# A graph attention layer walked in eight streams: the last tile's spreads of q put ahead of three one-hot tables, and the end's transfers shared out to POOL's queue

## The chip, the cores and the metric

The kernel runs on one core of a Trainium2 chip. Its engines work at the same time and wait for one another by semaphores: TensorE (PE in the profile) multiplies matrices into PSUM, VectorE (DVE) and ScalarE (ACT) work on SBUF and PSUM, GpSimd (POOL) and SyncE (SP) mostly issue transfers here. SP, ACT and POOL each issue transfers from a queue of their own. The metric is the time of one execution on the device in microseconds (us).

## The reference

One graph attention layer with a normalization ahead of it and the input added at its end: 12500 nodes of 256 numbers, 200000 edges sorted by destination, 8 heads of D = 32, everything in 32-bit floats.

```python
h = jnp.maximum(_layernorm(x, axis=-1), 0.0)
...
q = (x @ Wq + bq).reshape(n, HEADS, D)
k = (x @ Wk + bk).reshape(n, HEADS, D)
v = (x @ Wv + bv).reshape(n, HEADS, D)
logits = jnp.einsum('ehd,ehd->eh', q[dst], k[src]) / jnp.sqrt(jnp.float32(D))
seg_max = jax.ops.segment_max(logits, dst, num_segments=n)
expv = jnp.exp(logits - seg_max[dst])
denom = jax.ops.segment_sum(expv, dst, num_segments=n)
attn = expv / denom[dst]
agg = jax.ops.segment_sum(attn[:, :, None] * v[src], dst, num_segments=n)
out = agg.reshape(n, HID) + (x @ Wskip + bskip)
h = jax.nn.gelu(out, approximate=False)
y = x + h
```

The layer runs on h (its x is this h), y is normalized with gamma and beta, and the first x is added to it. The destinations are drawn as the square of a uniform number, so low nodes have many edges and high ones few.

## The kernel before

A first stage of some 205 us writes two tables to device memory: kv_tab, a row of 512 numbers (key and value) for each node, and h_tab, the normalized input. The change does not touch it.

The rest is `walk_streams`. The sorted edges are cut into S = 8 streams that are walked side by side. A step c takes K = 3 tiles of 128 edges from each stream, and there are 66 steps; the loop's body is written out 65 times (c = 0 to 64), and the last body breaks off halfway into the code of the end. Within a step the work on tile j goes as follows.

- Gather: for each of the 8 streams one indirect transfer on POOL's queue brings the 128 key and value rows of its edges (L1340, 262 KB). `gather_next` puts the 8 rows of a later tile on a list and has the first one issued behind a DVE instruction (`weigh`). The others are taken from the list one at a time by `turns(latest[PE])`, which stands behind each of the TensorE groups below: the gather then waits for that group's last matmul. When the list is empty, such a call does nothing. So the order in which TensorE's groups are written sets which gather waits for what.
- Windows and queries: `windows` fetches the 64 nodes that a stream may meet in this step from h_tab (SP), `turn_windows` transposes them (L1302, copied to hwT by ACT, L1306), and `queries` multiplies them with Wq (L1316, L1320, copied to qw by ACT, L1323).
- One-hot tables: `hot_e(c, i)` for i = 0 to 3 makes, by one matmul (L1366) and a relu on ACT (L1369), the table to_e of which edge belongs to which node of the window, two streams each. `hot_n` (L1379, L1382) makes the table for the way back.
- Spread: `spread(c, j, half)` multiplies qw with to_e (8 matmuls of 64 rows, L1392), so that each edge has its query, in one of two PSUM tiles ps_qe. Then `times` multiplies it with the gathered keys on DVE (L1402), `total` sums over a head's numbers (L1409), and `turn` transposes the logits (L1428).
- Softmax and sums: `maxima` runs two scans over the logits on DVE (L1440, L1441), ACT takes the exponential, `turn_back` transposes back (L1450), `weigh` multiplies the values (L1477), `add_up` sums them by node with to_n (L1500) and stores the sums to a table in device memory (L1522).

Tiles overlap: while step c is weighed and added up, the spreads and products of step c + 1 run, and the tables, queries and gathers of step c + 2 are made.

From a step on, `Pair`s of node blocks are finished beside the walk, one in each step (the first is due in step 18; the loop finishes one in 45 steps): `fetch` (sums, x and h by SP, L1056 to L1058), `turn`, `skip` and `add` (h times Wskip and the divided sums, in PSUM), `gelu` (ACT, L1097), `stats` and `root` (DVE, then a square root on ACT, L1113), in the next step `factors`, `normal`, `shifted`, `scale` and `store` (L1168). ACT loads a table (L1262) whenever it goes from one of gelu, square root and exponential to another.

Nothing schedules this: instructions run on each engine in the order in which the code is written. The piece of the loop's body that the change moves about is the middle one, between the first tile's `gather_next` and the second tile's.

At the end, after the last two steps, four `Half` pairs (`early_two` and `last`) and two whole ones (`before` and `older`) are left. A `Half` gets its rows in four pieces of 64 nodes, with one transfer each for h, x and sums (L1206, L1210, L1214) and one for each piece of the result. The sums of `last` can be fetched only when the last stores of the walk are done.

Of the kernel before, what the change touches and what calls it, by code (L numbers as in the profile page):

```python
# [38 lines left out]
DVE = mybir.EngineType.DVE  # L39
PSUM = bass.MemoryType.PSUM  # L40
DRAM = bass.MemoryType.DRAM

P = 128
# [943 lines left out]
def walk_streams(tc, N, HID, NST, KL, many, ident, idx, d0_row, slot_row, near, near_n, e_tab, pen_tab, h_tab,  # L987
# [39 lines left out]
    class Pair:  # L1027
# [4 lines left out]
        def __init__(self, pool, m, ps_h, ps_o, keep):  # L1032
            self.pool, self.m, self.ps_h, self.ps_o, self.keep = pool, m, ps_h, ps_o, keep

# [125 lines left out]

        def store(self, b, queue=nc.sync):
            if b == 0:
                self.nodes = loaded(slot_row[0:1, self.m, 0:2], N - P)
            self.put(out[ds(self.nodes[b], P), :], self.y[:, b, :], queue)
# [11 lines left out]
    class Half(Pair):  # L1176
# [26 lines left out]
        def fetch_h(self):  # L1203
            self.places()
            for t, node in zip(self.parts(self.h), self.nodes):
                self.keep(nc.sync.dma_start(t, self.rows_of(h_tab, node)))  # L1206
# [5 lines left out]
        def fetch_sums(self, group=None):  # L1212
            for t, row in zip(self.parts(self.sums), self.rows):
                ins = self.keep(nc.sync.dma_start(t, self.rows_of(tab, row)))  # L1214
                if group:
                    tc.add_to_no_dep_group(group, ins.ins)
# [11 lines left out]
    with ExitStack() as es:  # L1228
# [388 lines left out]
        for c in range(NST - 1):  # L1617
# [10 lines left out]
            if c == NST - 2:  # L1628
                last_nodes = places(0, N - P, (SP, ACT))
                last_rows = places(2, S * NT - P, (SP, ACT))  # L1630
# [60 lines left out]
            if pair:  # L1691
                table_of(AF.Gelu)
                pair.divide()
            if pair_next:
                pair_next.fetch()
            if before:
                before.store(1)
# [103 lines left out]
        last[0].fetch_x(nc.scalar)  # L1801
# [37 lines left out]
        for p in last:  # L1839
            p.shifted()  # L1840
        for p in [older] + done:
# [366 lines left out]
```

## Time and profile before

| | |
|---|---|
| median of 3 runs | 2704.53 us (2700.92 to 2709.87) |
| the profiled execution | 2724.49 us, its span 2722.4 us |
| mean granted clock of TensorE | 0.815 |
| busy, from 300 to 860 us (560 us) | PE 385.8, DVE 364.2, ACT 157.8, POOL 356.5 us |
| busy, from 1300 to 2500 us (1200 us) | PE 883.1, DVE 852.7, ACT 529.1, POOL 726.6 us |
| mean share of the DMA engines in these two | 0.70 and 0.75 |

The first stretch lies in the steps without a pair, the second in those with one. A row of the timeline gives the start, the duration, the engine, the line and the operation, and in brackets how long the engine idled just before and what ended it; "x16" are 16 instructions in one row. A row of a group (those with a "|") gives the total busy time and the mean of one in ns, then the idle time before all of them and the largest share of it by releaser.

### The profile page before, as it was taken

The page shows a single profiled execution, that of the slowest core. Times are in us where ns is not written, and L with a number is a line of the kernel's source. Part 1 is how long each engine was busy: PE and PEld are TensorE (multiplying, and loading weights), DVE is VectorE, ACT ScalarE, POOL GpSimd, SP SyncE. Part 2 cuts the span into 40 slices and gives each one's busy share as a digit, 9 for nine tenths or more (in the row PEclk, how much of TensorE's full clock was granted, in tenths as well). Part 3 has the DMA queues.
Part 4 walks back from the last instruction along what each step waited for, and adds up shares of the span by engine and source line. Part 5 has one row for each costly group of instructions (what it writes and reads, how often), then busy time and mean ns, then how long its engine had stood idle before and what let it go on. Part 6 is the DMA issues. An engine that isn't in the chain of part 4 may idle for free.

```text
span 2722.4 us, 36232 instructions
## 1 busy us (share of the span) xinstructions
PE 1982.6 (73%) x10159; PEld 1181.6 (43%) x10159; DVE 1869.3 (69%) x2165; ACT 1100.8 (40%) x2576; POOL 1620.4 (60%) x1741
## 2 busy tenths in 40 slices
PE   9994567677677677677766777777777777777776
PEld 4442344344444444444444444444444444444443
DVE  8872666666666667766767677776677767776776
ACT  5741222222222244444444444444444444444444
POOL 5456566666666665666556556656656666565652
PEclk9996777877777788888888887888888888888878
DMA  9786566777676777777777777777777777777773
GB/s 348 287 292 196 170 200 203 208 211 206 202 206 204 217 224 217 210 220 228 221 215 213 220 220 221 219 224 225 231 218 219 220 221 229 217 216 213 230 210 108
DMA packets 278904, 596.02 MB, mean 219 GB/s; under 512 B 53040, under 2 KB 166852, under 8 KB 275616
## 3 DMA queue, kind: packets, MB, share of 16 engines
q0 software_dynamic: 128224, 421.39, 53.5%
q1 hardware_dynamic: 148996, 170.91, 19.4%
q8 instruction: 83, 1.36, 0.2%
q10 hardware_dynamic: 1472, 1.31, 0.2%
q14 instruction: 129, 1.06, 0.1%
HBM read 510.92 MB, written 82.47 MB: 218 GB/s over the span
## 4 chain that ended last, share of the span: by engine, by line
PE 43%; another core or an unknown queue 14%; issue 13%; DVE 12%; ACT 11%; POOL 3%; DMA 2%; SPq 2%; DVEq 0%; POOLq 0%; ACTq 0%
PE ps_qe L1392 9%; PE ps_a L1088 6%; PE ps_a L1500 5%; PE ps_hot L1320 5%; ACT kv L1517 4%; DVE vw L1477 4%; PE ps_kv L340 4%; DVE kv L1402 3%; DVE L L1409 2%; PE ps_hot L1500 2%; POOL kv L1340 2%; ACT sums_w L1513 2%; ACT to_n L1382 2%; PE ps_hot L1153 2%
## 5 line engine op out<-in xcount | busy, mean ns | idle before, releaser
L1340 POOL DMA_INDIRECT kv<-kv_tab,idx x1520 | 1454.5, 957 | 926.3 <-issue 370.1
L1402 DVE TENSOR_TENSOR kv<-ps_qe,kv 128x1024 f32<-128x1024 f32 x392 | 466.6, 1219 | 587.5 <-remote 266.2
L1392 PE MATMUL ps_qe<-qw,to_e 64*128 64x256 f32 x3136 | 526.1, 476 | 216.2 <-issue 116.4
L1477 DVE TENSOR_TENSOR vw<-ps_x,kv 128x2048 f32<-128x2048 f32 x194 | 442.0, 2278 | 151.2 <-ACT vw L1466 123.7
L1392 PEld LDWEIGHTS ps_qe<-qw,to_e 64*128 64x128 f32 x3136 | 384.6, 234 | 370.8 <-issue 259.0
L1409 DVE TENSOR_REDUCE L<-kv 128x64 f32<-128x2048 f32 x196 | 447.7, 2284 | 5.1
L1323 ACT COPY qw<-ps_hot 128x256 f32<-128x256 f32 (+1 forms) x132 | 63.2, 479 | 601.6 <-PE ps_hot L1320 322.3
L1320 PE MATMUL ps_hot<-w_q,hwT 128*128 128x256 f32 x792 | 246.9, 456 | 19.2 <-ACT hwT L1306 18.8
L1500 PE MATMUL ps_a<-vw,to_n 128*32 128x264 f32 (+1 forms) x2304 | 237.0, 433 | 23.4 <-ACT kv L1517 18.3
L1320 PEld LDWEIGHTS ps_hot<-w_q,hwT 128*128 128x128 f32 x792 | 164.5, 222 | 117.7 <-issue 70.1
L1306 ACT COPY hwT<-ps_hot 128x256 f32<-128x256 f32 (+1 forms) x132 | 63.3, 480 | 360.4 <-PE ps_hot L1302 189.7
L340 PE MATMUL ps_kv<-w_kv,hT 128*128 128x512 f32 x392 | 184.5, 594 | 1.0 <-ACT hT L254 0.7
L1262 ACT ACT_TABLE_LOAD x139 | 178.3, 1283 | 2.6
L1088 PE MATMUL ps_a<-w_s,hT 128*128 128x256 f32 x360 | 167.7, 645 | 11.2 <-issue 4.8
L1379 PE MATMUL ps_hot<-near_n,et 48*128 48x384 bf16 x196 | 63.0, 376 | 143.3 <-ACT to_n L1382 139.3
L1366 PE MATMUL ps_hot<-et,near 48*128 48x384 bf16 x264 | 93.0, 353 | 91.7 <-ACT ps_x L1431 44.8
L1369 ACT ACTIVATE to_e<-ps_hot,ones 128x384 f32<-128x384 f32 x264 | 142.8, 581 | 10.4 <-PE ps_hot L1366 8.6
L1500 PEld LDWEIGHTS ps_a<-vw,to_n 128*32 128x32 f32 (+1 forms) x2304 | 95.2, 127 | 112.6 <-ACT kv L1517 39.6
L1517 ACT COPY kv<-ps_a 1x264 f32<-1x264 f32 x384 | 141.5, 368 | 6.3
L1088 PEld LDWEIGHTS ps_a<-w_s,hT 128*128 128x128 f32 x360 | 112.5, 328 | 58.7 <-issue 29.7
L1123 ACT ACTIVATE sums<-sums,nm,rstd 128x256 f32<-128x256 f32 x90 | 49.1, 592 | 211.0 <-DVE nm L1118 120.5
L1513 ACT COPY sums_w<-ps_a 128x264 f32<-128x264 f32 x128 | 48.4, 378 | 202.1 <-remote 74.7
(327 smaller groups left out, 2334.6 us busy)
## 6 DMA issues: line engine op xcount, KB each, us to landing
kv<-kv_tab,idx POOLq DMA_INDIRECT x1568
kv_tab<-kvo SPq DMA_DIRECT2D x23, 1024.0 KB
hw<-h_tab SPq DMA_DIRECT2D x264, 64.0 KB
table<-sums_w SPq DMA_DIRECT2D x260, 61.9 KB
pen<-pen_tab SPq DMA_DIRECT2D x66, 192.5 KB
sums<-table SPq DMA_DIRECT2D x92, 132.0 KB
x_in<-in_x_dram SPq DMA_DIRECT2D x23, 512.0 KB
h_tab<-h SPq DMA_DIRECT2D x23, 512.0 KB
```

Source lines behind the costliest of these rows:

```text
L340: nc.tensor.matmul(ps_kv, hT[:, c, :], w_kv[:, c, :], start=c == 0, stop=c == KC - 1)
L1088: self.keep(nc.tensor.matmul(self.ps[:, b, :], self.hT[:, b, c, :], w_s[:, c, :], start=False, stop=False, skip_group_check=True))
L1262: keep(nc.scalar.activation(dummy[:, 1:2], dummy[:, 0:1], function))
L1320: keep(nc.tensor.matmul(ps[:, b, :], g["hwT"][:, b, k, :], w_q[:, k, :], start=False, stop=k == KC - 1, skip_group_check=True))
L1340: ins = nc.gpsimd.indirect_dma_start(out=t[:, s, :], out_offset=None, in_=kv_tab[:, :], in_offset=bass.IndirectOffsetOnAxis(ap=idx[:, s, j ...
L1369: keep(nc.scalar.activation(step[c]["to_e"][:, i, :], ps[:, :CH], AF.Relu, scale=-1.0, bias=ones))
L1392: keep(nc.tensor.matmul(ps[:, b, a, :], g["to_e"][r, 2 * half + a, j * P:(j + 1) * P], g["qw"][r, (half + a) * half, :], start=True, stop= ...
L1402: keep(nc.vector.tensor_tensor(k, g["qe", half].rearrange("p b a d -> p a b d"), k, op=OP.mult))
L1409: keep(nc.vector.tensor_reduce(g["L"][:, j, :].rearrange("p (s h) -> p s h", s=S), g["kv"][j][:, :, :HID].rearrange("p s (h d) -> p s h d" ...
L1477: keep(engine.tensor_tensor(t[:, :, HEADS:].rearrange("p s (h d) -> p s h d", h=HEADS), wj[:, :, :, None].to_broadcast([P, t.shape[1], HEA ...
L1500: keep(nc.tensor.matmul(ps[at:at + w, :], g["to_n"][:, j, i * P + at:i * P + at + w], g["vw"][j][:, s, :], start=j == 0, stop=j == tiles_o ...
L1517: keep(copy(step[c + 1]["kv"][0][0:1, s, HID - HEADS:], ps[at:at + 1, :]))
```

## The change

In the walk's step, four things are written in another place. The store of the second block of a finished pair stands ahead of the next pair's fetches. `pair.add` stands behind the first queries, and `pair.gelu` behind the second ones. The three calls hot_e(c + 2, 1) to (c + 2, 3) stand behind the two spreads of the last tile of step c + 1. No instruction of the step is added or taken away.

The places in the list of gathers go with the order. For the first tile of step c + 2, row 0 still waits for `weigh`, and rows 1 to 5 for the first queries, `turn`, `turn_windows`, hot_e 0 and the second queries. Rows 6 and 7 waited for hot_e 1 and hot_e 2; they now wait for the first and the second half of the spread. The three calls behind them find the list empty.

At the end, several transfers change their queue: x of `last[0]` goes from ACT's to POOL's, x and sums of `last[1]` from SP's to POOL's, the eight stores of `early_two` from SP's to POOL's; of the eight stores of `last`, which SP and ACT had half each, SP has the four of `last[0]`, ACT and POOL two each of `last[1]`. The stores of `before` stand ahead of the fetches of sums of `last`, h of `last[1]` ahead of the sums of `early_two`; the loop around the gelus takes the pairs in another order, with `shifted` behind it; and the nodes that `before` and `older` are stored to are read earlier (`found`).

```diff
-            if pair_next:
-                pair_next.fetch()
             if before:
                 before.store(1)
-            if pair:
-                pair.add()
+            if pair_next:
+                pair_next.fetch()
             if c + 2 < NST:
                 queries(c + 2, 0)
             if pair:
-                pair.gelu()
+                pair.add()
             turn(c + 1, 0)
             if c + 2 < NST:
                 turn_windows(c + 2, 1)
                 hot_e(c + 2, 0)
                 queries(c + 2, 1)
-                for i in range(1, S // 2):
-                    hot_e(c + 2, i)
+            if pair:
+                pair.gelu()
             for half in range(2):
                 times(c + 1, 1, half)
                 spread(c + 1, K - 1, half)
+            if c + 2 < NST:
+                for i in range(1, S // 2):
+                    hot_e(c + 2, i)
             total(c + 1, 1)
...
+        last[1].fetch_h()
         for p in early_two:
             p.fetch_sums("whole")
-        last[1].fetch_h()
+        for p in (before, older):
+            p.found(keep)
...
-        last[0].fetch_x(nc.scalar)
+        last[0].fetch_x(nc.gpsimd)
...
-        last[1].fetch_x()
-        for p in last:
-            p.fetch_sums()
         for b in range(2):
             before.store(b)
+        last[0].fetch_sums()
+        last[1].fetch_sums(queue=nc.gpsimd)
+        last[1].fetch_x(nc.gpsimd)
...
-        for p in last:
-            p.shifted()
-        for p in [older] + done:
+        for p in (older, early_two[0], last[0], early_two[1], last[1]):
...
                 for part in range(2 if p is older else 4):
-                    p.store(part)
+                    p.store(part, nc.sync if p is older else nc.gpsimd)
+        for p in last:
+            p.shifted()
...
-                p.store(part, (nc.sync, nc.scalar)[part // 2])
+                p.store(part, nc.sync if p is last[0] else (nc.scalar, nc.gpsimd)[part // 2])
```

What this does to TensorE's order in a late step: first before, from the second queries (L1320) over the one-hot matmuls 1 to 3 (L1366, from the constant near and the step's et) to the two halves of the spread (L1392) and the transpose of logits (L1428). The loads of weights between them are left out.

```order
L1316 MATMUL ps_hot_9825<-b_q3_70,one_row_69 128x512
L1320 MATMUL ps_hot_9825<-w_q_68,hwT_9818 128x256 x4
L1366 MATMUL ps_hot_9833<-et_9572,near_84 128x384
L1366 MATMUL ps_hot_9837<-et_9572,near_84 128x384
L1366 MATMUL ps_hot_9841<-et_9572,near_84 128x384
L1392 MATMUL ps_qe_9845<-qw_9499,to_e_9518 128x256 x4
L1392 MATMUL ps_qe_9851<-qw_9499,to_e_9518 128x256 x4
L1428 MATMUL ps_x_2267<-ident_62,L_9770 64x128
```

The same place after, where five lines are added ahead in the file (L1325, L1371, L1397 and L1433 are those calls).

```order
L1321 MATMUL ps_hot_9824<-b_q3_70,one_row_69 128x512
L1325 MATMUL ps_hot_9824<-w_q_68,hwT_9817 128x256 x4
L1397 MATMUL ps_qe_9834<-qw_9497,to_e_9517 128x256 x4
L1397 MATMUL ps_qe_9841<-qw_9497,to_e_9517 128x256 x4
L1371 MATMUL ps_hot_9847<-et_9572,near_84 128x384
L1371 MATMUL ps_hot_9850<-et_9572,near_84 128x384
L1371 MATMUL ps_hot_9853<-et_9572,near_84 128x384
L1433 MATMUL ps_x_2267<-ident_62,L_9770 64x128
```

The spread, whose qw and to_e belong to the step before, comes right behind the queries, and the three one-hot matmuls stand between it and the transpose.

On ACT in the same step, before: the copies of the queries (qw) and of the transposed windows (hwT), the gelu (L1097), the relus that make to_e, and the square root (L1113) behind a table load.

```order
L1323 COPY qw<-ps_hot 128x256
L1097 ACTIVATE sums<-ps_a 128x512
L1431 COPY ps_x<-M 64x1
L1306 COPY hwT<-ps_hot 128x512
L1369 ACTIVATE to_e<-ps_hot,ones 128x384
L1323 COPY qw<-ps_hot 128x512
L1369 ACTIVATE to_e<-ps_hot,ones 128x384 x3
L1262 ACT_TABLE_LOAD
```

And after:

```order
L1328 COPY qw<-ps_hot 128x256
L1436 COPY ps_x<-M 64x1
L1311 COPY hwT<-ps_hot 128x512
L1374 ACTIVATE to_e<-ps_hot,ones 128x384
L1328 COPY qw<-ps_hot 128x512
L1099 ACTIVATE sums<-ps_a 128x512
L1374 ACTIVATE to_e<-ps_hot,ones 128x384 x3
L1267 ACT_TABLE_LOAD
```

The gelu has gone behind the copies that the second queries and the products wait for. The three relus keep their place in ACT's order, but the matmuls that they read now stand behind the spread.

More of the change, by code (lines that the diff above doesn't have):

```diff
@@ L39 @@
 DVE = mybir.EngineType.DVE
+POOL = mybir.EngineType.Pool
 PSUM = bass.MemoryType.PSUM
@@ L1033, in __init__ @@
             self.pool, self.m, self.ps_h, self.ps_o, self.keep = pool, m, ps_h, ps_o, keep
+            self.nodes = None
         def places(self):
@@ L1628, in walk_streams @@
             if c == NST - 2:
-                last_nodes = places(0, N - P, (SP, ACT))
-                last_rows = places(2, S * NT - P, (SP, ACT))
+                last_nodes = places(0, N - P, (SP, ACT, POOL))
+                last_rows = places(2, S * NT - P, (SP, POOL))
                 for each in (c, c + 1):
@@ L1693, in walk_streams @@
                 pair.divide()
+            if before:
+                before.store(1)
             if pair_next:
                 pair_next.fetch()
-            if before:
-                before.store(1)
-            if pair:
-                pair.add()
             if c + 2 < NST:
```

14 lines of the change are left out of this document (8 added, 6 removed).

## The prediction

> **What bounds the kernel now.** I read the page first: busy shares, chain, costliest groups.
>
> ```profile
> PE 1982.6 (73%) x10159; PEld 1181.6 (43%) x10159; DVE 1869.3 (69%) x2165; ACT 1100.8 (40%) x2576; POOL 1620.4 (60%) x1741
> PE 43%; another core or an unknown queue 14%; issue 13%; DVE 12%; ACT 11%; POOL 3%; DMA 2%; SPq 2%; DVEq 0%; POOLq 0%; ACTq 0%
> L1340 POOL DMA_INDIRECT kv<-kv_tab,idx x1520 | 1454.5, 957 | 926.3 <-issue 370.1
> L1402 DVE TENSOR_TENSOR kv<-ps_qe,kv 128x1024 f32<-128x1024 f32 x392 | 466.6, 1219 | 587.5 <-remote 266.2
> ```
>
> No engine is full. What stands out is line L1402, the products of gathered keys with spread queries: DVE idles 587.5 us ahead of it, and 266.2 us of that has no releaser the page can name ("remote"; on one core it means only that). So I went to the timeline of one late step, engine by engine.
>
> ```profile
> 1512.33 0.68 DVE L1100 TENSOR_TENSOR sums<-sums,h 128x512 f32<-128x512 f32 x1
> 1520.76 2.36 DVE L1402 TENSOR_TENSOR kv<-ps_qe,kv 128x1024 f32<-128x1024 f32 x2 [6.75 <-remote]
> 1523.04 0.15 DVE L1117 RECIPROCAL rstd<-rstd 128x2 f32<-128x2 f32 x1
> 1529.08 0.95 DVE L1440 TENSOR_TENSOR_SCAN ps_x<-pen,ps_x 64x384 f32<-64x384 f32 x1
> ```
>
> ```profile
> 1510.50 1.99 PE L1320 MATMUL ps_hot<-w_q,hwT 128*128 128x256 f32 x8
> 1512.42 0.33 PE L1366 MATMUL ps_hot<-et,near 48*128 48x384 bf16 x1
> 1513.65 0.32 PE L1366 MATMUL ps_hot<-et,near 48*128 48x384 bf16 x1 [0.16 <-issue]
> 1513.66 2.04 PE L1392 MATMUL ps_qe<-qw,to_e 64*128 64x256 f32 x16
> 1515.86 1.10 PE L1500 MATMUL ps_a<-vw,to_n 128*32 128x264 f32 x16
> 1522.04 3.76 PE L1392 MATMUL ps_qe<-qw,to_e 64*128 64x256 f32 x16 [5.09 <-DVE kv L1402]
> 1527.83 0.30 PE L1428 MATMUL ps_x<-ident,L 128*64 128x128 f32 x1 [0.44 <-DVE vw L1477]
> ```
>
> ```profile
> 1514.13 0.95 POOL L1340 DMA_INDIRECT kv<-kv_tab,idx  x1 [0.31 <-issue]
> 1515.38 0.95 POOL L1340 DMA_INDIRECT kv<-kv_tab,idx  x1 [0.30 <-issue]
> 1516.63 0.95 POOL L1340 DMA_INDIRECT kv<-kv_tab,idx  x1 [0.30 <-issue]
> 1517.88 0.95 POOL L1340 DMA_INDIRECT kv<-kv_tab,idx  x1 [0.30 <-issue]
> 1521.12 0.94 POOL L1340 DMA_INDIRECT kv<-kv_tab,idx  x1 [2.29 <-remote]
> 1524.40 0.95 POOL L1340 DMA_INDIRECT kv<-kv_tab,idx  x1 [1.08 <-PE ps_qe L1392]
> 1528.05 1.15 POOL L1340 DMA_INDIRECT kv<-kv_tab,idx  x1 [1.02 <-DVE vw L1477]
> ```
>
> The spread of the last tile (16 matmuls of 64 rows) is recorded from 1513.66 to 1515.70, yet DVE, with nothing else to do, takes up its products only at 1520.76, 7.1 us after that start. At about the same time POOL, which had issued gathers 1.25 us apart (0.95 and a 0.30 gap) and then waited, goes on (1521.12). The last gather of that burst ended at 1517.88 + 0.95 = 1518.83; DVE was released 1.93 us later. My reading is that such a spread is completed late while gathers are in flight, and is let go when POOL runs out of released rows and its queue drains. That is a reading, not a row.
>
> In the early steps, where no pair is finished, POOL's rows show the same beat without gaps:
>
> ```profile
> 566.65 0.94 POOL L1340 DMA_INDIRECT kv<-kv_tab,idx  x1 [2.10 <-remote]
> 578.40 0.95 POOL L1340 DMA_INDIRECT kv<-kv_tab,idx  x1 [2.05 <-remote]
> 587.16 0.95 POOL L1340 DMA_INDIRECT kv<-kv_tab,idx  x1 [0.30 <-issue]
> 590.19 0.95 POOL L1340 DMA_INDIRECT kv<-kv_tab,idx  x1 [2.08 <-PE ps_qe L1392]
> ```
>
> Eight gathers, a pause of 2.05 to 2.10, eight more. A step has 24 gathers: 24 x 1.25 + 3 x (2.07 - 0.30) = 35.3 us. The rows 566.65 and 590.19 lie 23.5 apart, two thirds of that. So early steps are bound by POOL's issuing plus three pauses; late ones by DVE's and TensorE's waits, with POOL having some slack.
>
> **The change, part by part: the walk's step.** Three things follow from the order shown above.
>
> (1) The spread goes ahead of three one-hot matmuls (hot_e). It would start at 1512.42 in place of 1513.66: 1.24 us earlier. The gelu leaves its place ahead of the copy of hwT on ACT, for which the query matmuls wait:
>
> ```profile
> 1508.98 0.60 ACT L1097 ACTIVATE sums<-ps_a 128x512 f32<-128x512 f32 x1
> 1509.47 0.16 ACT L1431 COPY ps_x<-M 64x1 f32<-64x1 f32 x1
> 1513.01 1.57 ACT L1369 ACTIVATE to_e<-ps_hot,ones 128x384 f32<-128x384 f32 x3
> 1514.60 1.28 ACT L1262 ACT_TABLE_LOAD   x1
> 1516.01 0.28 ACT L1113 ACTIVATE rstd<-mv,eps 128x2 f32<-128x2 f32 x1
> ```
>
> That is another 0.49 (1508.98 to 1509.47): 1.73 together. DVE's statistics (1512.33) then wait about a microsecond for the gelu, in time in which DVE idles 6.75 now: nothing, as long as that wait stays above 1 us. pair.add moves behind the first queries on TensorE, the store of an output row ahead of six fetches on SP: the gelu reads the former 3 us later than now, the fetched rows are for the next step. Both nothing.
>
> (2) Rows of the gather queue are released one by one by TensorE instructions as they are written. For the tile being gathered, rows 6 and 7 are released now by hot_e 1 and 2; afterwards by the two halves of the spread. POOL's rows at 1515.38 and 1516.63 are these, and 1517.88 (the next tile's row 0) queues behind them. So POOL's burst ends three gathers earlier, 3 x 1.25 = 3.75 us, at 1515.08; with the same 1.93 the release comes at 1517.0, not 1520.76. Three gathers are left for later: POOL has issued them by 1517.3 + 3 x 1.25 = 1521.0, where it starts the next row now (1521.12). POOL loses nothing there.
>
> (3) hot_e 1 to 3 come behind the late spread, and with them their three relus on ACT, and behind these a table load and the root. The second half of the spread is done some 1.0 after the first (half of 2.04): 1518.0. Then 1.57 for the relus, 1.41 from table load to root (1514.60 to 1516.01), 0.28: the root is there at 1521.3. DVE's reciprocal of it stands at 1523.04 now, and comes right behind the products. So of the 3.75 us only 1.7 are left at that point.
>
> (4) Next on TensorE comes add_up (1515.86 now), then the next step's first spread (1522.04 now). It can start when add_up is through: 1519.0 for the last hot_e, 0.3 for the transpose, 1.1, so 1520.4, 1.6 earlier. But it now starts with gathers in flight, where before it had POOL's pause. Its neighbours bound this: as released at 1524.40 now (first half 2.1 us after its start with two gathers in flight) the 1.6 are kept; late as the other spread is, until POOL waits for it and drains, it is done near 1526.5, not 1525.8, and the transpose at 1527.83, on which the scan at 1529.08 depends, comes 0.8 later. I take 0.8 us gained: the row at 1524.40 is the nearest (the same spread), with half of its gain taken off for three more gathers in flight. Ends: -1.7 and +0.8.
>
> Steps that finish a pair: 45. 45 x -0.8 = -36 (ends -77 and +36).
>
> Early steps, 18: POOL bounds them, so only its pauses count. Rows 6 and 7 behind the spread move a pause from behind the next tile's row 0 to ahead of row 6. If the next spread then needs no pause of its own, it stays at three: 0. One more costs 2.05 - 0.30 = 1.75 a step; the earlier release may give up to 1.0. I take 0 (ends -18 and +32), since the beat of three pauses is what the rows show.
>
> **The end.** SP issues its transfers one after the other:
>
> ```profile
> 2694.61 2.51 SPq L1210 DMA_DIRECT2D kv<-in_x_dram  x4
> 2697.45 5.10 SPq L1214 DMA_DIRECT2D kv<-table  x8
> 2708.90 8.98 SPq L1168 DMA_DIRECT2D out_dram<-kv  x12
> 2712.32 0.87 DVE L1143 SCALAR_TENSOR_TENSOR kv<-kv,rstd_l,ps_hot 128x256 f32<-128x256 f32 x2
> ```
>
> Four x rows and four of the eight sums leave SP for POOL, two stores of another pair come ahead: 2.5 + 2.5 - 1.3 = 3.7 us less of issuing ahead of the last sums on SP. POOL issues its four, waits for the stores to land, and its price for a plain transfer has no row; the nearest is the gather's 1.25: 5.0 for four against SP's 2.6, so the last half's sums are about 1 us earlier at best. The final twelve stores on SP: the early pairs' eight, which lie ahead of the last ones now, go to POOL, and SP keeps four. SP ends at 2717.88, 4.7 after DVE's last result (2713.19), and would end some 2.6 after it (four stores at 0.65). Together -4.5; ends -7 (both in full) and +2 (POOL's eight early stores, at 1.25 each, still run when the last two come).
>
> **Sum.** 2724.5 (the profiled execution's time; its span is 2722.4) - 36 + 0 - 4.5 = 2684. The median of the runs shown is 20 lower, so 2664.
>
> **Rivals.**
> A, the full gain: nothing is given back in (4), and early steps gain 1.0: -77 - 18 - 4.5 = -99.5, 2605. For it: the next spread takes 3.76 after an idle 5.09, against 2.04 for the same work at 1513.66; with less idling it may run as the other does. "TensorE: Matmul & The Clock Gate" of the Trainium skill, section "What's actually happening", puts the halved clock behind an idle window of about 3.4 us; by that rule a wait cut to 3 us would leave the spread at 2.04. Against it: POOL must still fit 24 gathers and its pauses in the step.
>
> B, the lateness is not POOL's doing: the release stays 7.1 after the spread's start and comes 1.73 earlier, at 1519.0; by (3) the root is then there at 1523.3, behind the 1523.04 of now: nothing gained, 2700 with the end. For it: 7.1 us is one step's distance only; both readings fit that step. The Trainium skill's page "SBUF — State Buffer", section "Who interferes with whom", says a transfer never contends with a compute engine; by that rule gathers cannot hold up matmuls, and this is the case to expect. The trace speaks against it as far as times go: the release follows the end of POOL's burst.
>
> C, slower: the pause that the spread needs is taken twice. The next step's first spread becomes as late as the last tile's is now, since gathers never stop in between; rows 3 and 4 of the next tile wait for it, POOL pauses a fourth time. Late steps +0.8, early +1.75: 36 + 32 - 4.5 = +63, 2768. It decides as soon as that spread ends later than POOL's row at 1524.40, plus what is saved ahead of it. For it: early steps have no slack on POOL, and the spread there sits in a pause now.
>
> **Chances.** My forecast 0.40, A 0.17, B 0.14, C 0.29. B is within 0.3% (8 us, about what can be told from no change), so are the edges of the forecast: faster 0.57, same 0.11, slower 0.32. Range 2590 to 2765: it takes in most of A and of C; the forecast's own is 2630 to 2695.
>
> **What would show it.** Right: the wait ahead of L1402 behind the last tile's spread falls from 6.75 to about 3, POOL pauses ahead of row 6 and no more at 1521; "remote" ahead of L1402 falls well below 266; the reciprocal L1117 waits for ACT. B: the release stays 7 us behind the spread's start, POOL idling longer. C: new gaps of 2 us on POOL released by the spread, and waits ahead of the scans. I am wrong altogether if late completion has another cause that the new order brings to other matmuls.

## The result and the profile after

The changed kernel takes 2711.21 us (median of 15 runs, 2697.55 to 2723.18); the kernel before, in runs beside it, 2705.01 us (15 runs, 2696.33 to 2712.05). The ratio is 1.0031 with an interval of 1.0019 to 1.0043: slower by 0.2 to 0.4%. I had said 2664 us and faster.

The traces must be compared with care: the profiled execution of before was 20 us above its median, that of after (2714.36 us, span 2712.7) 3 us above its own. The spans differ by -9.7 us, the medians by +6. So what follows reads where waits sit, and leaves it to the experiments to say what they are worth.

The page of after: busy shares, chain, and three groups.

```profile
PE 1943.7 (72%) x10159; PEld 1173.7 (43%) x10159; DVE 1874.0 (69%) x2165; ACT 1110.3 (41%) x2576; POOL 1627.4 (60%) x1763
PE 39%; another core or an unknown queue 16%; DVE 14%; ACT 13%; issue 13%; DMA 2%; POOL 2%; SPq 0%; DVEq 0%; POOLq 0%; ACTq 0%
L1345 POOL DMA_INDIRECT kv<-kv_tab,idx x1520 | 1450.7, 954 | 921.8 <-issue 363.3
L1407 DVE TENSOR_TENSOR kv<-ps_qe,kv 128x1024 f32<-128x1024 f32 x392 | 463.8, 1219 | 329.0 <-PE ps_qe L1397 168.8
L1482 DVE TENSOR_TENSOR vw<-ps_x,kv 128x2048 f32<-128x2048 f32 x194 | 442.0, 2279 | 249.3 <-ACT vw L1471 247.8
```

L1097 to L1117 of before stand two lines lower down here, and all from L1168 on five: L1345 is the gather that was L1340, L1407 the products that were L1402. The idle time ahead of the products fell from 587.5 to 329.0 us, as the change would have it. POOL's idle time ahead of the gathers is nearly what it was: 926.3 before, 921.8 now. Where DVE's 258 us went is in its list of waits (what waits, what it waits for: us in total, times, longest):

```profile
DVE vw L1482 <- ACT vw L1471: 247.8, 62, 6.9
DVE kv L1407 <- PE ps_qe L1397: 168.8, 53, 6.2
DVE kv L1407 <- remote: 98.8, 32, 33.5
DVE sums L1102 <- issue: 75.2, 30, 3.3
DVE sums L1102 <- ACT qw L1328: 35.9, 12, 3.5
DVE sums L1102 <- ACT sums L1099: 8.7, 3, 3.3
```

The weighing (L1482) waits 249 us, for the copy of the transposed weights on ACT, and the pair's statistics (L1102), which wait for the gelu, 120 us (75.2 + 35.9 + 8.7). In before the weighing waited 151 us:

```profile
L1477 DVE TENSOR_TENSOR vw<-ps_x,kv 128x2048 f32<-128x2048 f32 x194 | 442.0, 2278 | 151.2 <-ACT vw L1466 123.7
```

"Remote" fell from 266.2 to 98.8, as foretold, and the run did not get shorter: the wait is now elsewhere.

One late step of after, TensorE first, then POOL, ACT and DVE:

```profile
1512.33 1.99 PE L1325 MATMUL ps_hot<-w_q,hwT 128*128 128x256 f32 x8
1514.25 2.00 PE L1397 MATMUL ps_qe<-qw,to_e 64*128 64x256 f32 x16
1520.80 3.38 PE L1397 MATMUL ps_qe<-qw,to_e 64*128 64x256 f32 x16 [0.93 <-issue]
```

```profile
1514.35 0.95 POOL L1345 DMA_INDIRECT kv<-kv_tab,idx  x1 [0.30 <-issue]
1516.92 0.94 POOL L1345 DMA_INDIRECT kv<-kv_tab,idx  x1 [1.62 <-PE ps_hot L1371]
```

```profile
1516.68 0.59 ACT L1328 COPY qw<-ps_hot 128x512 f32<-128x512 f32 x1 [4.22 <-PE ps_hot L1371]
1517.16 0.60 ACT L1099 ACTIVATE sums<-ps_a 128x512 f32<-128x512 f32 x1
1517.65 1.71 ACT L1374 ACTIVATE to_e<-ps_hot,ones 128x384 f32<-128x384 f32 x3
1517.80 0.69 DVE L1102 TENSOR_TENSOR sums<-sums,h 128x512 f32<-128x512 f32 x1 [3.07 <-ACT qw L1328]
1519.52 2.36 DVE L1407 TENSOR_TENSOR kv<-ps_qe,kv 128x1024 f32<-128x1024 f32 x2
```

The query matmuls are recorded to end at 1514.32, but the copy of their result on ACT starts at 1516.68, 2.4 us later, and POOL's next row, which the same matmuls release, waits with it (1516.92, after a gap). The gelu now stands behind that copy, so it and the statistics are late with it. Behind the statistics come the products, at 1519.52, though their spread is recorded to end at 1516.25. The lateness has not gone. It has moved from the spread to the queries ahead of it.

In before these queries are on time. The prediction's row of them (L1320) ends at 1510.50 + 1.99 = 1512.49, and the copy starts 0.04 us later:

```profile
1512.53 0.58 ACT L1323 COPY qw<-ps_hot 128x512 f32<-128x512 f32 x1 [1.91 <-issue]
```

POOL was issuing gathers 1.25 us apart at that moment too (1510.20, 1511.45, 1512.71). So a gather being issued is not enough to make a result late.

### The profile page after: what moved, and what is told of

The parts are those of the page before. It is cut to its first block, busy times and chain, and to the rows that moved or that the text cites. A ratio compares the mean times of both kernels' runs of the same rounds, so it can differ in the third digit from the quotient of the medians.

```text
span 2712.7 us, 36198 instructions
## 1 busy us (share of the span) xinstructions
PE 1943.7 (72%) x10159; PEld 1173.7 (43%) x10159; DVE 1874.0 (69%) x2165; ACT 1110.3 (41%) x2576; POOL 1627.4 (60%) x1763
## 4 chain that ended last, share of the span: by engine, by line
PE 39%; another core or an unknown queue 16%; DVE 14%; ACT 13%; issue 13%; DMA 2%; POOL 2%; SPq 0%; DVEq 0%; POOLq 0%; ACTq 0%
PE ps_qe L1397 9%; PE ps_a L1090 6%; PE ps_hot L1325 6%; ACT kv L1522 6%; DVE vw L1482 5%; PE ps_kv L341 4%; DVE L L1414 4%; PE ps_a L1505 3%; DVE kv L1407 3%; ACT sums_w L1518 2%; PE ps_hot L1073 2%; ACT to_n L1387 2%; PE ps_hot L1384 1%; PE ps_hot L1371 1%
## 5 line engine op out<-in xcount | busy, mean ns | idle before, releaser
L1345 POOL DMA_INDIRECT kv<-kv_tab,idx x1520 | 1450.7, 954 | 921.8 <-issue 363.3
L1407 DVE TENSOR_TENSOR kv<-ps_qe,kv 128x1024 f32<-128x1024 f32 x392 | 463.8, 1219 | 329.0 <-PE ps_qe L1397 168.8
L1482 DVE TENSOR_TENSOR vw<-ps_x,kv 128x2048 f32<-128x2048 f32 x194 | 442.0, 2279 | 249.3 <-ACT vw L1471 247.8
L1397 PE MATMUL ps_qe<-qw,to_e 64*128 64x256 f32 x3136 | 522.8, 484 | 27.0 <-issue 25.1
L1397 PEld LDWEIGHTS ps_qe<-qw,to_e 64*128 64x128 f32 x3136 | 384.9, 245 | 214.9 <-issue 159.2
L1325 PE MATMUL ps_hot<-w_q,hwT 128*128 128x256 f32 x792 | 246.0, 455 | 18.7 <-ACT hwT L1311 18.5
L1371 PE MATMUL ps_hot<-et,near 48*128 48x384 bf16 x264 | 83.5, 334 | 204.9 <-issue 112.7
L1455 PE MATMUL ps_x<-ident,W 64*128 64x64 f32 x195 | 33.9, 301 | 259.6 <-issue 135.8
L1325 PEld LDWEIGHTS ps_hot<-w_q,hwT 128*128 128x128 f32 x792 | 163.6, 221 | 120.1 <-issue 72.3
L1455 PEld LDWEIGHTS ps_x<-ident,W 64*128 64x128 f32 x195 | 22.8, 185 | 290.2 <-issue 151.8
L1384 PE MATMUL ps_hot<-near_n,et 48*128 48x384 bf16 x196 | 78.8, 465 | 85.1 <-ACT to_n L1387 82.8
```

Of the source, the lines that this page charges most:

```text
L1325: keep(nc.tensor.matmul(ps[:, b, :], g["hwT"][:, b, k, :], w_q[:, k, :], start=False, stop=k == KC - 1, skip_group_check=True))
L1345: ins = nc.gpsimd.indirect_dma_start(out=t[:, s, :], out_offset=None, in_=kv_tab[:, :], in_offset=bass.IndirectOffsetOnAxis(ap=idx[:, s, j ...
L1397: keep(nc.tensor.matmul(ps[:, b, a, :], g["to_e"][r, 2 * half + a, j * P:(j + 1) * P], g["qw"][r, (half + a) * half, :], start=True, stop= ...
L1407: keep(nc.vector.tensor_tensor(k, g["qe", half].rearrange("p b a d -> p a b d"), k, op=OP.mult))
L1482: keep(engine.tensor_tensor(t[:, :, HEADS:].rearrange("p s (h d) -> p s h d", h=HEADS), wj[:, :, :, None].to_broadcast([P, t.shape[1], HEA ...
```

## The experiments

**How they are read.** All kernels were timed beside the kernel before on the same chip. Chips turned out to be of two kinds, whatever the kernel: on four (A, of the result above; B, C and D) before takes 2703 to 2728 us, on two (E and F) 2241 and 2242. On E and F POOL never pauses. The trace of before on F, the spread and the first of its products:

```profile
1502.69 2.04 PE L1392 MATMUL ps_qe<-qw,to_e 64*128 64x256 f32 x16
1503.91 1.23 DVE L1402 TENSOR_TENSOR kv<-ps_qe,kv 128x1024 f32<-128x1024 f32 x1 [0.33 <-issue]
L1340 POOL DMA_INDIRECT kv<-kv_tab,idx x1520 | 1451.3, 955 | 463.3 <-issue 224.0
```

The products start 1.2 us after the spread's start, not 7.1, and POOL, whose gathers take the same time (1451 us, 1454 on A), idles 463 us in place of 926.

The granted clock differs as well: 0.89 to 0.91 as a mean in the traces of E and F, 0.81 to 0.82 in those of the others (0.76 in no_turns_3, below). As recorded, it does not explain why the spread of the prediction is late. First the stretch of before on A in which that spread is recorded (the columns are PE, PEld, DVE, ACT and POOL busy, then the granted clock, the DMA engines' share and GB/s), then one on F with a spread and its products:

```profile
1515.00:1517.00 2.00, 1.96 (x24) 0.82 (x21) 0.00 (x0) 1.97 (x4) 1.39 (x3) 1.00 0.82 234
1525.00:1527.00 2.00, 2.00 (x10) 1.31 (x10) 0.00 (x0) 0.00 (x0) 1.39 (x3) 0.50 0.87 262
1525.43 2.91 PE L1392 MATMUL ps_qe<-qw,to_e 64*128 64x256 f32 x16
1527.53 2.36 DVE L1402 TENSOR_TENSOR kv<-ps_qe,kv 128x1024 f32<-128x1024 f32 x2 [3.27 <-PE ps_qe L1392]
```

On A the clock is 1.00 (from 1513 us on) and the products start 7.1 us after the spread's start. On F it is 0.50 and they start 2.1 us after it.

I worked out from POOL's rows of each trace the mean time of a step and the part of it in which POOL pauses (gaps over 0.5 us between gathers, less the usual 0.30). 24 gathers 1.2525 us apart are 30.06 us, and a step is about that plus its pauses. This sum holds by the way it is counted, whatever engine sets the pace; the table tells where time is lost, not why. Each line is one trace:

```
                        step, us          pauses, us
                     early    late      early    late      (early: steps 4 to 17, late: 21 to 60)
A  before            35.64    38.10      5.62    7.78
A  after             35.90    37.81      5.79    7.56
B  end_only          35.67    38.27      5.64    7.93      (its walk is that of before)
B  walk_only         36.44    37.87      6.27    7.70
B  hot_only          36.22    38.99      6.04    8.69
B  gelu_only         35.59    37.98      5.50    7.52
C  small_rows_3      35.23    37.72      5.18    7.33
C  no_turns_3        45.09    46.71     14.99   16.44
D  gelu_end_2        35.23    37.79      5.12    7.35
D  after_3           35.98    37.81      5.85    7.52
D  two_pops_3        35.31    37.97      5.28    7.59
E, F  six kernels   ~30.05   30.25 to 30.39     0        0
```

There are 18 early steps (without a pair) and 46 late ones.

**Theory and rivals.** After the result my theory was: a step costs POOL's issuing plus pauses that late TensorE results force on it; the change moves where POOL pauses and leaves their sum. Rivals: the order on ACT took the gain (the gelu behind the copy, the relus ahead of the root); the bytes in flight make the results late; the end lost what the walk gained.

### Walk or end

walk_only has the new walk's step with the end of before; end_only the reverse.

> The walk's step as changed, the end as before. The whole change measured +0.3% (2711 against 2705). Pause theory: POOL's step is 24 gathers of 1.25 us plus the pauses in which a spread that was begun among gathers gets done; the change moves these pauses and does not shorten them (POOL's idle time ahead of gathers went from 926 to 922 us over the run). The end should be worth -4 (from the last scan to the end of the span 47.0 us before, 43.1 after), so the walk alone is slower by more than the whole: 2712 to 2721. Rival: the end is what costs, and the walk alone is at 2700 to 2706.

> The end as changed, the walk's step as before. Pause theory (the walk costs, the end gains): 2699 to 2703, from the last scan to the end 42 to 44 us in place of 47. Rival (the end costs, POOL's transfers are dear): 2708 to 2715.

On B, where before takes 2728.0: walk_only 2727.64, ratio 1.0001 (0.9985 to 1.0016); end_only 2727.08, 0.9987 (0.9973 to 1.0). The end is worth some -3.5 us (0 to -7.4 by the interval), as expected; the walk's step nothing (within 4 us), where my theory had it 0.3 to 0.6% slower. What fits it is the range of the rival (2700 to 2706, beside 2705). That nothing is a sum, as the table shows: late steps are 0.40 us shorter (46 x -0.40 = -18), early ones 0.77 longer (18 x 0.77 = +14).

### Which half of the walk's step

hot_only moves the three one-hot matmuls and leaves the rest of the step as before; gelu_only moves all the rest and leaves these three ahead of the spreads.

```diff
                 queries(c + 2, 1)
-                for i in range(1, S // 2):
-                    hot_e(c + 2, i)
             for half in range(2):
                 times(c + 1, 1, half)
                 spread(c + 1, K - 1, half)
+            if c + 2 < NST:
+                for i in range(1, S // 2):
+                    hot_e(c + 2, i)
```

```diff
-            if pair_next:
-                pair_next.fetch()
             if before:
                 before.store(1)
-            if pair:
-                pair.add()
+            if pair_next:
+                pair_next.fetch()
             if c + 2 < NST:
                 queries(c + 2, 0)
             if pair:
-                pair.gelu()
+                pair.add()
...
                 queries(c + 2, 1)
+            if pair:
+                pair.gelu()
+            if c + 2 < NST:
                 for i in range(1, S // 2):
```

> Of the change only the three one-hot matmuls behind the two spreads; gelu, add and the store stand as before. Pause theory: 2700 to 2718, POOL's idle time ahead of gathers within 15 us of 926; the wait goes from the statistics back to the products. Rival (ACT's order is the loss: with the gelu behind the late copy of qw DVE waited 116 us ahead of the statistics, L1102): that wait is gone and the kernel is at 2600 to 2660.

> Of the change only the gelu, the add and the store in their new places; the one-hot matmuls stand ahead of the spreads as before. Pause theory: nothing, 2700 to 2710; the copy of qw is on time since no spread follows the queries directly, DVE waits for the gelu inside its idle time. Rival (ACT's order is the loss): 2712 to 2725.

hot_only: 2772.51, ratio 1.0168 (1.0151 to 1.0186). gelu_only: 2711.94, 0.9947 (0.993 to 0.9964). So the spread ahead of the three tables, for which the change is named, costs 45 us by itself; what gains is the gelu's new place with pair.add and the store, about 15. The rival that blames the gelu's place on ACT is out by this; the relus ahead of the root are in what follows. Neither the theory nor its rival had foretold either number, and the pauses' sum does not stay: it rises by 0.76 us a late step in hot_only and falls by 0.41 in gelu_only (7.93 in end_only). In the trace of hot_only the pair's root is late, as step (3) of the prediction had it:

```profile
1500.62 1.73 ACT L1369 ACTIVATE to_e<-ps_hot,ones 128x384 f32<-128x384 f32 x3 [6.26 <-remote]
1504.08 0.17 DVE L1117 RECIPROCAL rstd<-rstd 128x2 f32<-128x2 f32 x1 [2.27 <-ACT rstd L1113]
DVE rstd L1117 <- ACT rstd L1113: 92.9, 41, 2.3
L1340 POOL DMA_INDIRECT kv<-kv_tab,idx x1520 | 1454.4, 957 | 975.0 <-issue 311.0
```

The three relus start at 1500.62, the table load and the root follow, and DVE waits 2.27 us for it, in 41 steps (92.9 us in all). Of this the table's late steps lose 0.72 x 46 = 33 us, and the early ones, which have no root, 0.55 x 18 = 10: 43 of the 45. With the gelu moved as well (walk_only beside gelu_only) the late steps lose nothing more from the move (37.87 and 37.98), the early ones still 0.85.

Why early steps lose shows in POOL's list of waits from 300 to 860 us. First walk_only, then gelu_only, then end_only:

```profile
POOL kv L1340 <- PE ps_hot L1320: 25.1, 10, 2.8
POOL kv L1340 <- PE ps_qe L1392: 10.8, 10, 2.6
```

```profile
POOL kv L1340 <- PE ps_qe L1392: 16.5, 18, 2.1
```

```profile
POOL kv L1345 <- PE ps_qe L1397: 16.0, 17, 2.5
POOL kv L1345 <- PE ps_hot L1325: 2.8, 1, 2.8
```

With the three tables behind the spread, POOL pauses ten times, 2.5 us each, for the second query matmuls (L1320), which end_only shows once and gelu_only not among its largest. hot_only has 21.2 us of it (9 times). It is a pause at a place that I had not named. Pauses ahead of other rows move or shrink at the same time, so the 0.77 is the sum of several. It is not a late result in the sense above: in these early steps the copy of the second queries starts 0.04 us (median) behind their recorded end in every kernel of the list, so the matmuls themselves come later.

In late steps gelu_only also shows that the queries are not late because a spread comes right behind them: its three tables lie in between, and the copy is late all the same, 2.7 us after the recorded end (1471.17).

```profile
1469.18 1.99 PE L1320 MATMUL ps_hot<-w_q,hwT 128*128 128x256 f32 x8
1473.86 0.59 ACT L1323 COPY qw<-ps_hot 128x512 f32<-128x512 f32 x1 [4.55 <-remote]
```

hot_only is the counterpart: there the spread does come right behind the queries, and the copy is on time. From 1300 to 2500 us its median distance from the recorded end is 0.04 us in before, end_only and hot_only, and 2.4 to 2.5 us in after, walk_only, gelu_only and gelu_end_2. So the queries became late with the half that moves pair.add, the gelu and the store, which is the half that gains. Which of the three does it was not tried.

### The gaining halves together

gelu_end is the changed kernel with the three tables back ahead of the spreads. It went on E and, as gelu_end_2, on D beside after_3, which is the changed kernel itself; after_again is that on F.

```diff
-            for half in range(2):
-                times(c + 1, 1, half)
-                spread(c + 1, K - 1, half)
             if c + 2 < NST:
                 for i in range(1, S // 2):
                     hot_e(c + 2, i)
+            for half in range(2):
+                times(c + 1, 1, half)
+                spread(c + 1, K - 1, half)
```

> The change without its move of the one-hot matmuls: gelu, add and store in their new places, and the end as changed. The two parts alone measured 0.9947 and 0.9987 of before. If they add: 0.9934, some 18 us faster than before. If the gain of the first was the beat of that build alone: 0.997 to 1.002.

> The change without the move of the one-hot matmuls. On a chip with late spreads, if the parts add: 0.9934 of before (0.9947 for the gelu's move, 0.9987 for the end). If the first was the beat of that build: 0.997 to 1.002. On a chip without late spreads 0.9971, as before.

> The whole change, beside it on the same chip. With late spreads 1.001 to 1.005 of before (1.0031 on record), so 0.7 to 1.1% slower than without the move of the one-hot matmuls. Without late spreads 0.9971, the same as its neighbour.

> The changed kernel, unchanged. On a chip like the first (before near 2710 to 2730): the pauses move and their sum stays within 0.5 us a step, 0.999 to 1.005 of before. On a chip like the second (before near 2242): no spread is late, POOL issues without a pause and the walk's order is worth nothing; the end gives 0.3%: 0.995 to 0.999.

On D, where before takes 2703.2: gelu_end_2 2694.1, 0.9961 (0.9948 to 0.9974); after_3 2708.49, 1.0013 (0.9999 to 1.0028). They differ by 14.4 us, and the table says where: late steps are alike (37.79 and 37.81), early ones differ by 0.75, 18 x 0.75 = 13.5. (The two traces as a whole differ by 3.6 us only: the profiled execution of gelu_end_2 took 2704.88, 10.8 above its median, and loses 5.9 us to after_3 behind the last gather.) On E gelu_end has 0.9971 (0.996 to 0.9982), on F after_again the same 0.9971 (0.9959 to 0.9983), some 6 us: where POOL never pauses, the three tables' place is worth nothing. What is left I take to be the end's; single traces do not settle it, since from the last gather to the end of the span before_again takes 62.7 us and after_again 57.9, but no_turns, whose end is that of before, 56.6. On D gelu_end_2 is faster than the changed kernel, on E and F the two have the same ratio, and gelu_only on B had a lower one still (0.9947, with an interval that overlaps): that the changed end adds to the gelu's gain is not shown. gelu_end_2 gains less than its halves added up (0.9947 x 0.9987 = 0.9934); those were measured on B, and I did not find where the rest, some 7 us, goes.

### What makes the results late

small_rows gathers 64 numbers in place of a row of 512, an eighth of the bytes with as many transfers and rows. It leaves out the rest of each row (the buffers are zeroed once), and its 64 numbers come from the wrong place, the first eighth of the table, so it does not compute the layer.

```diff
+        kv_64 = kv_tab[:, :].rearrange("n (a d) -> (n a) d", d=64)
...
-                    out=t[:, s, :], out_offset=None, in_=kv_tab[:, :],
+                    out=t[:, s, :64], out_offset=None, in_=kv_64[:, :],
```

no_turns releases a tile's eight rows to POOL at once in place of one by one; two_pops releases two in place of one behind the transposes of the weights.

```diff
                 waiting.extend((t, c + 2, j, s) for s in range(S))
-                turns(latest[DVE])
+                turns(latest[DVE], S)
```

```diff
-            turns(latest[PE])
+            turns(latest[PE], 2)
```

> The kernel before, but each gather brings rows of 64 numbers in place of 512 (the first 64 places of the edge's row, from the wrong place of the table; the other places of six fixed buffers stay zero, set once by VectorE): the same 24 gathers and as much issuing on POOL, an eighth of the bytes. Pause theory, with the lateness due to the bytes in flight: the products' idle time on DVE (L1402, 587 us, 266 of it 'remote') falls below 250, POOL's pauses fall from 5.6 to 7.8 us a step to under 4, the run to 2350 to 2550 us. Lateness due to POOL's issuing or the number of descriptors, or TensorE's own: the idle time stays above 500 and the run at 2620 to 2710.

> The kernel before, but all eight rows of a tile are released at once, behind the DVE instruction that released the first: no gather waits for a TensorE group. Pause theory: POOL issues eight in a row without a look at TensorE, spreads and queries begun meanwhile are late until the burst is drained, the pauses stay (5 to 8 us a step, now behind DVE): 2690 to 2800. Rival (the pauses are only POOL waiting for its turn, and cost by themselves): the pauses shrink to 1 to 3 us a step and the run to 2450 to 2600.

> The kernel before, but the transpose of the weights (L1450) releases two rows in place of one, so that the last row of the third tile no longer waits for the second tile's spread, where POOL paused 2.8 us in each of 40 late steps. Pause theory: the pause is needed, that spread or what is ahead of it becomes late and POOL pauses elsewhere, sum 7 to 8.5 us a late step: 2695 to 2740. Rival (this pause is POOL's alone): the sum falls by 1.5 to 2.8 a late step, the run by 70 to 125 us.

These first went on E, where POOL never pauses, and tell only what the edits cost there: small_rows 2255.86 beside 2242.46, no_turns 0.9994 (0.9985 to 1.0004), two_pops 1.0 (0.9991 to 1.0009). On F the picture is the same: small_rows_2 2253.43 beside 2241.11, no_turns_2 1.0004 (0.9995 to 1.0013), before_again 2243.84.

> Again the eighth of the bytes by as many gathers; in the first run, on a chip where nothing was late, it took 2256 us against 2242. On a chip with late spreads: if bytes in flight make them late, the pauses go and the run is at 2240 to 2400; if POOL's issuing or TensorE itself does, the pauses stay and the run is above 2600. On a chip without: 2240 to 2270 again, and nothing is told.

> Again all eight rows released at once by DVE; 0.9994 of before on a chip where nothing was late. On a chip with late spreads, pause theory: the pauses stay, now behind DVE, within 2% of before. Rival (pauses are only POOL's waiting for its turn): under 0.95 of before. On a chip without: 0.998 to 1.001 again.

> The kernel before once more, unchanged, for a trace of it beside the other runs of this call: the first calls ran on chips where it took 2728 and 2242 us. On a chip like the first, steps of 35.5 and 38 us with 5.6 and 7.8 us of POOL pauses; on one like the second, steps of 30.0 to 30.4 us without pauses. No third kind is expected.

Then on C, where before takes 2703.16, one run each, and two_pops_3 on D:

> The eighth of the bytes by as many gathers, a third time, in the hope of a chip with late spreads. There: if bytes in flight make spreads late, the pauses go and the run is at 2240 to 2400; if POOL's issuing or TensorE itself does, the pauses stay and the run is above 2600. On a chip without late spreads: 2240 to 2270.

> All eight rows released at once by DVE, a third time. On a chip with late spreads, pause theory: the pauses stay, now behind DVE, within 2% of before. Rival (pauses are only POOL's waiting for its turn): under 0.95 of before. On a chip without: as before within 0.3%.

> The transpose of the weights releases two rows in place of one. With late spreads, pause theory: the 2.8 us pause ahead of the third tile's last row goes, others grow, 7 to 8.5 us a late step, 0.996 to 1.013 of before. Rival (this pause is POOL's alone): 0.955 to 0.975. Without late spreads 1.000, as before.

small_rows_3 takes 2706.92. Its page, and one stretch of 40 us with the columns as above:

```profile
L1351 POOL DMA_INDIRECT kv<-kv_tab,idx x1520 | 1458.1, 959 | 896.5 <-issue 380.7
L1413 DVE TENSOR_TENSOR kv<-ps_qe,kv 128x1024 f32<-128x1024 f32 x392 | 468.4, 1219 | 552.7 <-PE ps_qe L1403 230.0
1500.00:1540.00 40.00, 30.99 (x165) 18.79 (x161) 28.83 (x30) 16.86 (x38) 24.39 (x26) 0.83 0.31 81
```

The DMA engines are busy 0.31 of the time here (before: 0.75 from 1300 to 2500 us), and DVE still idles 552.7 us ahead of the products, POOL 896.5 ahead of the gathers. Even if the 12 to 13 us that the edit costs on E and F are taken off, the bytes are worth some 10 of the 460 us that lie between the two kinds of chip, no more than single runs scatter (before on A: 2696 to 2712).

no_turns_3 takes 3290.32 us, 587 more, where the same kernel costs nothing on E and F. Neither the theory's range (within 2% of before) nor the rival's came true. POOL's rows show its bursts (1.25 us apart) and the waits between them:

```profile
L1340 POOL DMA_INDIRECT kv<-kv_tab,idx x1520 | 1459.3, 960 | 1479.5 <-issue 490.8
1514.90 0.95 POOL L1340 DMA_INDIRECT kv<-kv_tab,idx  x1 [6.76 <-ACT dummy L1262]
1544.25 1.15 POOL L1340 DMA_INDIRECT kv<-kv_tab,idx  x1 [8.07 <-DVE vw L1477]
```

The pauses grew to 15 us a step early and 16 late (5.6 and 7.8 in before on A): as I read it, a product waits for its spread until the burst is over, and the next burst is released by that product. So on this chip fewer bytes save next to nothing and longer bursts cost much. I conclude that the lateness goes with POOL's issuing of indirect transfers and not with what they carry; that is argued from two single runs, and the punctual queries of before show that issuing alone does not suffice. What in it does this (POOL's work on the descriptors, the rows' number, the queue) was not separated, nor why only some chips have it.

two_pops_3 is 2715.53, 1.0039 (1.0026 to 1.0052). The release that it brings forward takes away the late step's pause of 2.8 us ahead of the third tile's last row, and the step's sum of pauses stays where the other kernels' is, 7.59. That is the theory's plainest case: the pause comes back two rows later, ahead of the next tile's second row, where 0.72 us a step in before (on A) become 3.46. That row waits for TensorE too, for the first queries; whether TensorE needs POOL's pause, or is late by itself and POOL only waits, this run cannot tell. The 10 us that it costs I could not put down to a row.

## Why the prediction was wrong, step by step

Of the picture of what bounds the kernel this much stood: E and F, where POOL never pauses, run a late step in 30.25 to 30.39 us, which is the 30.06 of the issuing and little else; on the other chips pauses come on top, early and late. Lateness beside POOL's issuing turned out not to be general: the queries of before are on time. What I took from the picture did not stand. The step that failed is the one from an earlier release to a shorter step, (2) and (4) below.

**Step (1).** The spread did come right behind the queries, and "remote" fell below 100. The statistics' wait for the gelu was mis-sized: I set it to a microsecond because I took the copy of the queries ahead of it as punctual. It was so in the old order and is late in the new one, and the statistics wait 3.07 in the step shown and 120 us over the run. The time was not lost there, though. gelu_only, the fastest kernel on B, has 130 us of the same wait:

```profile
DVE sums L1100 <- ACT qw L1323: 98.9, 31, 3.4
DVE sums L1100 <- ACT sums L1097: 31.0, 10, 4.7
```

**Step (2).** POOL's burst did end earlier, even one row ahead of what I had worked out, and the release came with POOL's pause. "POOL loses nothing there" is the sentence that failed. I let three gathers slide into slack that I took from one row (1521.12). The sum of the pauses is what a late step is made of, and it fell by 0.2 us (7.78 to 7.56 on A, 7.93 to 7.70 on B), not by what the spread gained.

**Step (3).** The late root is real: 2.27 us in 41 steps of hot_only, where I had worked out 1.9 (1521.3 against products that end at 1519.4). In the changed kernel the statistics are late themselves, and the root waits less for the relus.

**Step (4) and the sum.** For late steps I took -0.8, with ends -1.7 and +0.8; B has -0.40, 46 x -0.40 = -18 in place of -36, and what earned most of it is the half with the gelu (-0.29 in gelu_only), not the spread's place. For early steps I took 0 and named +1.75 for one more pause; B has +0.77, 18 x 0.77 = +14: rival C's pause in the early steps, taken for the queries and not for the first spread. So -36 + 0 came out as -18 + 14.

**The end.** -4.5 lies inside what was measured: from the walk's last scans to the span's end the traces have 47.0 us before and 43.1 after, and end_only gave -3.5 (0 to -7.4). The price of POOL's plain transfers, which I bounded by the gather's 1.25 us, is 0.53 to 0.6; the rows of after:

```profile
2690.04 1.72 POOL L1219 DMA_DIRECT2D kv<-table  x3
2694.56 3.62 POOL L1173 DMA_DIRECT2D out_dram<-kv  x6 [0.21 <-DVE den_l L1067]
2704.63 0.87 DVE L1145 SCALAR_TENSOR_TENSOR kv<-kv,rstd_l,ps_hot 128x256 f32<-128x256 f32 x2
2704.10 2.80 SPq L1173 DMA_DIRECT2D out_dram<-kv  x4
2705.80 1.05 POOL L1173 DMA_DIRECT2D out_dram<-kv  x2 [6.04 <-DVE kv L1145]
```

Three take 1.72, six 3.62, two 1.05. SP ends at 2706.90, 1.4 after DVE's last result (2705.50); I had said 2.6.

**The rivals.** A's full gain did not come: the pauses stayed. Its clock rule ("TensorE: Matmul & The Clock Gate" of the Trainium skill, "What's actually happening") would have let the next spread run in 2.04 us once the wait ahead of it fell below 3.4; in the step shown its recorded wait fell to 0.93, and it took 3.38. B's ground, the rule of "SBUF — State Buffer" of the Trainium skill, "Who interferes with whom", that a transfer never contends with a compute engine, agrees with small_rows_3 as to the bytes. B's reading that the lateness is not POOL's doing does not go well with no_turns_3. B's time, 2700, came nearest, by luck: its release 7.1 us after the spread's start did not stay (1519.52 - 1514.25 = 5.3). C was half of what happened, in the early steps.

**What does not close.** The walk at 0 and the end at -3.5 on B would put the changed kernel 3.5 below before; it measured 6 us above on A and 5 above or none on D (1.0013, 0.9999 to 1.0028). Some 7 to 10 us are lost where the two parts meet, or between chips. The intervals of the two parts, some 4 us each way, cover a good part of it. As walk and end were never measured apart on A or D, this stays open.

## What to carry to other kernels

Where a step's time is one engine's issuing plus its pauses, ask of a reordering whether the sum of the pauses falls: here earlier releases mostly moved the pauses, and the group of waits that shrinks most (587 to 329 us here) says nothing until the waits that grew are added. Nor is a wait that grows a loss by itself: the 130 us in gelu_only went with a gain. A releaser that was punctual at its old place in the order (the copy of the queries, 0.04 us) need not be so at its new one (2.4 us). Of a change that bundles several moves, time each half alone: here one half gained 15 us, the other lost 45 alone, and the two together came out at nothing, as the first covers most of the second's loss.

## What was unexpected of the hardware

One program takes 2703 to 2728 us on four chips and 2241 or 2242 on two. On the latter the mean granted clock is 0.89 to 0.91 (0.81 to 0.82 in most traces of the others), the products follow their spread at 1.2 us at full clock and 2.1 us at half clock in the steps shown, and POOL never pauses. On the slower four, some results of TensorE reach the engines that wait for them up to 5 us after the recorded end, full-size matmuls (2.4 us in the step of after) as well as those of 64 rows, and others at once: the same query matmuls are on time in before and late in gelu_only. "Perfetto Trace Analysis" of the Trainium skill, "Tensor Engine Instruction (MATMUL, LD_WEIGHTS)", says that the end of a matmul's record is estimated, not observed; the rows here agree, since the spread recorded to end at 1515.70 in before let DVE go at 1520.76.
